# A scan's second sweep on silu in PSUM and on the state itself, with smaller pieces in the tail, in a cross-attention kernel

## The chip, the core and the metric

The kernel runs on one core of a Trainium2 chip, in float32. The time is that of one execution on the device, in microseconds (us); the times below are the median of repeated runs. Inputs lie in the chip's memory before the kernel starts, and the output is written there. The engines are called PE (TensorE, matrix products), DVE (VectorE), ACT (ScalarE), POOL (GpSimd) and SP (SyncE, which only issues transfers).

## What is computed

```python
x  = layernorm(builder_state, g1, beta1);  base_n = layernorm(base_state, g1, beta1)
x  = builder_state + mha(x, base_n, W_qkv, b_qkv, W_o, b_o)      # 8 heads of 64, softmax
xn = layernorm(x, g2, beta2)
U  = (xn @ W_in.T + b_in) @ Bmat                                  # 64 numbers a row
def step(s, u_t):
    s = silu(s @ A.T) + u_t
    return (s, s)
_, states = scan(step, zeros, U)                                  # over the rows, state of 64
out = x + states @ Cmat + (program_probs.mean(1) @ W_prog.T + b_prog)
```

There are 4096 rows of 512 and 3202 rows of keys. The last two lines are the part that the change touches.

## The kernel before

**Attention.** The rows are taken in eight blocks of 512. For each block and each pair of heads PE makes scores, ACT their exponentials, DVE adds these up, and PE multiplies them with the values; the products of several heads are then projected and normalised. The rows of a finished block are kept (`x1` in memory with the residual, `u` = U in SBUF). The last 256 rows come last: their four pairs of projection products `yb` (one bank for each of two row tiles, `last` in the plan), then `l.x1`, statistics, turning and `l.kept` for each tile.

**The scan.** Chunks of the 4096 rows run side by side: 16 steps, each on a 128x128 tile that holds 64 states of 256 chunks in two halves. The first sweep `a` starts each chunk from zero and gives the states at the chunks' ends (`end1`); the second sweep `b` starts each chunk from the end of the chunk ahead, and its states are what goes to the output. The influence of an older state fades within a chunk, and at the end the program tests that: the new ends `end0` are compared with `end1` (`differ b`), and only if an element differs by more than `TOL` (2^-21) times its row's largest does a general branch recompute everything (`tc.If(n > 0)`). The last 256 rows have a scan of their own, 20 steps on 128x32 tiles (`l.terms` puts their inputs through A, `l.z` is the product on PE, `l.h` the silu on ACT), which is compared too (`differ l`).

**How a step of a sweep is written.** Silu is written there as z/2 * (tanh(z/2) + 1). `terms` puts four steps' inputs through A into a bank ahead of time, `z` adds A times h of the step before, ACT takes the tanh, DVE makes h, which is the state without its input. In sweep `b` POOL adds the input (`states`, s = h + u), and the product with `Cmat` (`products`, four matmuls, in two column pieces of 256) gives the row's output for both halves into two banks. One half is joined with the row on DVE (`joined0`); the other is copied by ACT out of PSUM and added by POOL in two rows of three (`copied`, `added`), and joined on DVE in the third (`joined1`). Then both are stored. There are two pairs of banks, rows with even and odd number.

**What sets the order.** All of it is a list of pieces with an engine, a cost, what they come after, and a due date. `Plan.order` simulates the engines and takes on each the piece with the earliest due date that can run; the instructions are emitted in that order, and each engine runs its own in that order. The due dates are moved by the table `SHIFT` (in units of 2.15 us), an entry for each sort of piece. A piece that waits on its engine keeps the ones behind it waiting.

The names in the rows of order and profile: `z` and `za` are the banks of the sweeps, `zl` the banks of the 20 steps (the last one lies in `py_o`), `scan` the tile that holds h, s, tanh and the ends, `c_14613` and `a_t` what multiplies them, `py_o`, `py_n` and `pd_last` the output banks (`py_o` and `py_n` one pair, both halves of `pd_last` the other), `row` the row that is joined and stored, `y_l` its copy.

Of the kernel before, what the change touches and what calls it, by code (L numbers as in the profile page):

```python
# [10 lines left out]
F32 = mybir.dt.float32  # L11
# [25 lines left out]
WARM = 17  # L37
# [39 lines left out]
class Plan:  # L77
# [19 lines left out]
        "a": -42, "add": 137.25, "add.h": 196.75, "add.l": -10, "added": -29.75, "b": 2.5, "base": -5.25,  # L97
        "c2": -6.5, "close": -19, "copied": 70.25, "den": 113.25, "den.h": -32.5, "den.l": -73.25,
        "differ": -272.25, "extra": -26.25, "fall": -8.25, "fall.h": 160.75, "fall.l": 77, "fetch": 41.25,
        "fold.h": 108.75, "fold.l": 39.5, "gather": 180, "gather.h": 4.25, "gather.l": -116.5, "got": 47,  # L100
        "heads": 4, "held": -43.25, "inverse": 45.5, "inverse.h": -19.5, "inverse.l": 54, "join": -69.5,
        "join.h": -34.75, "join.l": 117.25, "joined0": -182.75, "joined1": 53, "l.copy": 43,
        "l.factors": -49.5, "l.from": -46.75, "l.h": 8, "l.idle": 264, "l.inputs": -15.75, "l.kept": -22.25,
        "l.mod": -99.25, "l.out": -7, "l.scaled": -35.75, "l.states": -41.5, "l.stats": 258.75,
        "l.store": 0.25, "l.terms": -7, "l.turn": 1, "l.x1": 16.25, "l.ys": 89.25, "l.z": -4.75, "landed": -6,
        "last": 2.25, "maximum": 76.5, "number": -17.5, "open": -0.75, "output.h": 18.25, "output.l": -14.25,
        "outs": 2.5, "outs.read": -6.75, "product": -4.25, "products": -5.75, "py1": -8.25, "q": 116,
        "query.factors": -34, "query.flip": 197, "query.load": -145.5, "query.move0": -72,
        "query.move1": 94.5, "query.move2": 13, "query.move3": 1, "query.scaled": 154.75, "query.stats": 42.5,
        "rest": -21.25, "rest.h": 110, "rest.l": -53.25, "rise": 17.25, "risen": -66.5, "row.copy": -12,  # L110
        "row.factors": -129, "row.flip": 0.75, "row.kept": -5.5, "row.load": -3.5, "row.mod": -207.5,
# [16 lines left out]
    def add(self, name, engine, cost, run, after=(), due=0, take=(), give=(), kind=None, also=0):  # L128
        assert name not in self.pieces, name
        sort = name if isinstance(name, str) else name[0]  # L130
        if sort in ("row", "query", "rows", "queries"):
            sort += "." + name[-1]
        elif sort in self.UNIT and name[1] >= self.HALVES:
            sort += ".l" if name[1] >= self.ENDS else ".h"
# [2740 lines left out]
```

## Time and profile before

| what | value |
| --- | --- |
| three runs | 1869.35, 1869.7, 1871.12 us; median 1869.7 |
| profiled execution | 1871.54 us, span on the core 1869.7 us |
| granted clock of TensorE, mean | 0.999 |
| busy over the span | PE 1853.6 (99%), DVE 1496.3 (80%), ACT 1143.1 (61%), POOL 306.0 (16%) us |
| last block's attention ends, tail begins | about 1819.5 us |
| length of the tail | 50.2 us, of which 6.7 after the last output on DVE |

The span runs from the first to the last instruction of the profiled execution, and every position in the text is counted from its start. The 99% of PE is a mean over the whole kernel, in which the tail is less than 3%. The change lies in the tail and in what is emitted just ahead of it, so the stages of the tail have to be read one by one.

### The profile page before, as it was taken

The numbers are of one execution on the slowest core, as the hardware profiler recorded it, in microseconds if no ns is written. First come the engines' busy times: TensorE is split into PE (matmuls) and PEld (weight loads), VectorE is DVE, ScalarE is ACT, GpSimd is POOL, SyncE is SP. The second block draws the span as 40 slices with busy tenths as digits, with TensorE's granted clock in tenths as the row PEclk, the third lists the DMA queues.
The fourth block names the chain that finished last, engine by engine and source line by source line (L and its number), as shares of the span: only waits on it lengthen the run. The fifth ranks groups of instructions, "written<-read, shape, count | busy, mean of one in ns | idle before, by whom it ended". The sixth has DMA issues, their size and how long they took to land.

```text
span 1869.7 us, 44352 instructions
## 1 busy us (share of the span) xinstructions
PE 1853.6 (99%) x17956; PEld 926.7 (50%) x17956; DVE 1496.3 (80%) x1734; ACT 1143.1 (61%) x1409; POOL 306.0 (16%) x395
## 2 busy tenths in 40 slices
PE   9999999999999999999999999999999999999997
PEld 5888334534353433434343435344343434577674
DVE  6642688688888889798979888888979897888776
ACT  3242577575757667575756575766757575757653
POOL 6120300021100130022102110023002210020115
PEclk9999999999999999999999999999999999999999
DMA  8663242331424233413333132423331342535577
GB/s 258 161 169 89 65 117 58 83 111 54 112 74 139 57 105 100 115 48 88 108 85 121 52 108 80 139 58 106 100 112 50 82 112 85 155 111 171 159 194 238
DMA packets 262704, 206.90 MB, mean 111 GB/s; under 512 B 95759, under 2 KB 235935, under 8 KB 262497
## 3 DMA queue, kind: packets, MB, share of 16 engines
q1 hardware_dynamic: 258476, 197.41, 37.2%
q10 hardware_dynamic: 4020, 6.62, 1.3%
q8 instruction: 143, 2.34, 0.5%
q14 instruction: 65, 0.52, 0.1%
HBM read 157.24 MB, written 29.89 MB: 100 GB/s over the span
## 4 chain that ended last, share of the span: by engine, by line
PE 97%; DVE 1%; SPq 1%; DMA 0%; ACT 0%; issue 0%; POOL 0%; ACTq 0%; DVEq 0%
PE po L1406 32%; PE s L1300 32%; PE po L1431 5%; PE s L1313 5%; PE qx L523 3%; PE pax L523 3%; PE qy L523 2%; PE pay L523 2%; PE pkx L523 2%; PE pvx L523 2%; PE pky L523 1%; PE pvy L523 1%; PE pk L863 1%; PE pv L736 1%; PE pd L1460 1%; PE pu L1920 1%
## 5 line engine op out<-in xcount | busy, mean ns | idle before, releaser
L1344 ACT ACTIVATE p<-s,shifts 128x1024 f32<-128x1024 f32 x804 | 886.2, 1110 | 437.9 <-PE s L1300 361.2
L1352 DVE TENSOR_TENSOR acc<-p,acc 128x1024 f32<-128x1024 f32 (+1 forms) x732 | 916.5, 1257 | 81.3 <-ACT p L1344 51.5
L1406 PE MATMUL po<-p,v 64*64 64x512 f32 x5600 | 730.4, 590 | 0.0
L1300 PE MATMUL s<-q,k 64*64 64x512 f32 x5600 | 729.0, 589 | 0.0
L1300 PEld LDWEIGHTS s<-q,k 64*64 64x64 f32 x5600 | 217.8, 133 | 371.1 <-issue 333.5
L1406 PEld LDWEIGHTS po<-p,v 64*64 64x64 f32 x5600 | 217.5, 133 | 360.1 <-issue 341.7
L1807 POOL TENSOR_TENSOR xr<-xr,rowb 128x512 f32<-128x512 f32 x28 | 35.7, 1276 | 793.0 <-DVE acc L1352 682.2
L1518 DVE RECIPROCAL rd<-rd 128x256 f32<-128x256 f32 (+1 forms) x64 | 109.9, 1718 | 29.7 <-ACT rd L1513 29.6
L1431 PE MATMUL po<-p,v 64*64 64x256 f32 x1600 | 107.3, 377 | 0.0
L1313 PE MATMUL s<-q,k 64*64 64x256 f32 x1600 | 106.8, 377 | 0.0
L1902 POOL TENSOR_TENSOR xr<-x,modb 128x512 f32<-128x512 f32 x28 | 35.4, 1274 | 317.2 <-DVE acc L1380 228.7
L1313 PEld LDWEIGHTS s<-q,k 64*64 64x64 f32 x1600 | 64.1, 133 | 25.1 <-issue 3.2
L1431 PEld LDWEIGHTS po<-p,v 64*64 64x64 f32 x1600 | 64.4, 133 | 21.5 <-issue 1.9
L1352 DVE TENSOR_TENSOR acc<-p,p 128x1024 f32<-128x1024 f32 x36 | 44.0, 1223 | 19.4 <-ACT p L1344 19.3
L1375 ACT COPY swap<-acc 64x512 f32<-64x512 f32 (+1 forms) x70 | 40.2, 574 | 18.8 <-DVE acc L1352 16.2
L1738 ACT ACTIVATE q<-qx,bias 128x256 f32<-128x256 f32 x42 | 17.6, 471 | 52.7 <-PE qx L523 52.7
L1588 POOL TENSOR_SCALAR rstd_x<-mv_x 128x1 f32<-128x1 f32 x28 | 24.7, 882 | 146.3 <-DVE mv_x L1585 144.6
L719 DVE TENSOR_TENSOR ks<-pky,ks 128x512 f32<-128x512 f32 x15 | 10.4, 692 | 45.0 <-PE pky L523 24.6
L1380 DVE TENSOR_TENSOR acc<-swap,acc 64x512 f32<-64x512 f32 (+1 forms) x70 | 44.1, 630 | 1.1
L713 ACT ACTIVATE ks<-pkx,bias 128x256 f32<-128x256 f32 x40 | 16.8, 471 | 43.8 <-PE pkx L523 26.6
L440 DVE TENSOR_REDUCE m<-ex 128x2 f32<-128x1024 f32 (+1 forms) x9 | 9.9, 1101 | 39.9 <-ACT ex L436 39.9
L1590 POOL TENSOR_SCALAR nm_x<-mv_x,rstd_x 128x1 f32<-128x1 f32 x28 | 34.9, 1246 | 2.8
(325 smaller groups left out, 1749.5 us busy)
## 6 DMA issues: line engine op xcount, KB each, us to landing
k<-kd SPq DMA_DIRECT2D x432, 128.0 KB, 2.6
v<-vd SPq DMA_DIRECT2D x432, 128.0 KB, 2.5
xn<-x SPq DMA_DIRECT2D x448, 32.0 KB, 1.9
xr<-in_x_dram SPq DMA_DIRECT2D x30, 256.0 KB, 4.1
x1d<-xr SPq DMA_DIRECT2D x30, 256.0 KB, 3.2
x<-in_x_dram SPq DMA_DIRECT2D x28, 256.0 KB, 3.2
cx<-in_ctx_dram SPq DMA_DIRECT2D x25, 256.0 KB, 4.0
kd<-ks SPq DMA_DIRECT2D x20, 256.0 KB, 4.9
```

The lines of the kernel that those rows point to most:

```text
L523: nc.tensor.matmul(to[:, b, :], still[:, i, b * P : (b + 1) * P], moving[:, i, :], start=(start and b == 0 and i == 0), stop=(i == 1), ski ...
L1300: nc.tensor.matmul(s[k0 : k0 + HD, a].rearrange("p b j -> p (b j)"), kts[(*w["at"][:2], c // 2)][r, b * CK + k0 : b * CK + k0 + HD], q[r], ...
L1313: nc.tensor.matmul(s[k0 : k0 + HD, a, b, :], kts[(*w["at"][:2], c)][r, b * CK + k0 : b * CK + k0 + HD], q[r], start=True, stop=True, skip_ ...
L1344: nc.scalar.activation(t[:, :, :nb, :], w["ps"][c][:, :, :nb, :], AF.Exp, bias=w["shift"])
L1352: return nc.vector.tensor_tensor(w["acc"][:, :, :nb, :], t[:, :, :nb, :], before[:, :, :nb, :], ALU.add)
L1375: nc.scalar.copy(w["swap"][r], of[(1 - k) * HD : (2 - k) * HD])
L1380: made = nc.vector.tensor_tensor(of[r], w["swap"][r], of[r], ALU.add)
L1406: nc.tensor.matmul(w["po"][k][a * HD : (a + 1) * HD], vts[Q, hp, c // 2][r, c % 2, a * HD : (a + 1) * HD], t[r, a].rearrange("p b j -> p ( ...
L1431: nc.tensor.matmul(w["po"][k][a * HD : (a + 1) * HD, :QU], vts[Q, hp, c][r, b, a * HD : (a + 1) * HD], t[r, a, b, :], start=(c == 0 and b ...
L1518: nc.vector.reciprocal(w["rd"][:, part], (w["pd"] if last else w["rd"])[:, part])
L1807: return nc.gpsimd.tensor_tensor(xs[half][:, t], xs[half][:, t], rowb, ALU.add)
L1902: return nc.gpsimd.tensor_tensor(xt[:, t], x1[:, t], modb, ALU.add)
```

## The change

- The second sweep becomes `second_sweep`. A step is: `z` = A times the whole state (no `terms`), ACT's Silu in place in PSUM, and one DVE operation s = 2 * silu + u. The state goes into one of four buffers, the last one directly into `end0`; `states` on POOL and `b.end` are gone. `z` of a step waits for the state of the step before, in place of h.
- `products` are made in four column pieces of 128, `copied` in two halves of 256 columns, each after its two pieces of the products.
- `l.terms` is made in five pieces, the four `l.idle` pairs of matmuls (which computed nothing) are gone.
- `differ` is one piece on DVE, with the absolute value as max(d, -d); it was three, the middle one on ACT.
- `l.mod` waits for `l.scaled` of the second tile, where it waited for `l.factors`. A transposed copy in the last block's last rows takes another tile (`xn2` goes). The pace of sweep `b` in the due dates is 1500 for 1900.
- `SHIFT` has entries of their own for the rows of the last block (`.e`) and for the four `last`, and nearly all its numbers for the tail are others. The order on PE is the same as before up to the third last of the 36 units of attention work.
- The general branch uses `second_sweep` too.

```diff
     SHIFT = {
-        "a": -42, "add": 137.25, "add.h": 196.75, "add.l": -10, "added": -29.75, "b": 2.5, "base": -5.25,
+        "a": 39.25, "add": 137.25, "add.h": 487.75, "add.l": 19.25, "added": -59, "b": -188.25, "base": -5.25,
...
+    def second_sweep(start, d=0, pace=0, after=()):
+
+        k = "b"
+
+        def at_(j):
+            return sv["z"][j // 4 % 2][:, j % 4, :]
+
+        def z_(j):
+            on_a(at_(j), state(j - 1) if j else sv[start][:, :NCK], start=True)
+
+        def silu_(j):
+            nc.scalar.activation(at_(j), at_(j), AF.Silu)
+
+        def s_(j):
+            nc.vector.scalar_tensor_tensor(state(j), at_(j), 2.0, u[:, j, :], ALU.mult, ALU.add)
+
+        for j in range(L):
+            yield (k, "z", j), "PE", 260, partial(z_, j), [(k, "s", j - 1)] if j else list(after), d, [], [], "quarters"
+            yield (k, "silu", j), "ACT", 280, partial(silu_, j), [(k, "z", j)] + ([] if j else ["table"]), d + 400
+            free = [("products", j - 4, part) for part in range(NC)] if j > 3 else []
+            yield (k, "s", j), "DVE", 290, partial(s_, j), [(k, "silu", j)] + free, d + 800
+            d += pace
...
-        def copied():
-            nc.scalar.activation(sv["y"][:, j % 2, :], sv["py"][j % 2][1], AF.Copy, scale=0.5)
+        def copied(half):
+            hs = slice(half * QU, (half + 1) * QU)
+            nc.scalar.activation(sv["y"][:, j % 2, hs], sv["py"][j % 2][1][:, hs], AF.Copy, scale=0.5)
...
-        nc.scalar.activation(df, df, AF.Abs)
+        nc.vector.scalar_tensor_tensor(df, df, -1.0, df, ALU.mult, ALU.max)
...
-            plan.add(("l.mod", g), "POOL", 1250, partial(mod_, g), [("l.x1", g), ("l.factors", 1)],
+            plan.add(("l.mod", g), "POOL", 1250, partial(mod_, g), [("l.x1", g), ("l.scaled", 1)],
...
-        for t in range(WARM, PRE + LT):
-            plan.add(("l.idle", t), "PE", 430, idle_, [("l.z", t), ("b", "h", L - 1)], d)
...
-            plan.add(("states", j), "POOL", 450, lambda j=j: states(j, sv["h"][j % 3]),
-                     [("b", "h", j)] + ([("products", j - 2, part) for part in range(2)] if j > 1 else []), e)
-            for part in range(2):
-                plan.add(("products", j, part), "PE", 450, partial(products_, j, part),
-                         [("states", j), *free[j % 2]], e + 1000 + part, [], [], "quarters")
+            for part in range(NC):
+                plan.add(("products", j, part), "PE", 225, partial(products_, j, part),
+                         [("b", "s", j), *free[j % 2]], e + 1000 + part, [], [], "quarters")
```

PE from the last attention products (`po`) to the end of the projection (`yb`), before. The `z` rows are sweep `b`, with `z<-u` its `terms`; `yb_17647` and `yb_17648` are row tile 0 and 1, `o_0_0` and `o_2_0` what is projected:

```order
L1431 MATMUL po_7_3_1_17388<-p_3_1_12_17529,v_3_1_12_17357 64x256
L2133 MATMUL z<-scan,a_t 64x128 x2
L2133 MATMUL z<-u,a_t 64x384 x2
L2285 MATMUL yb_17647<-wo,o_0_0_15077 128x512
L2285 MATMUL yb_17648<-wo,o_0_0_15077 128x512
L2285 MATMUL yb_17647<-wo,o_0_0_15077 128x512
L2285 MATMUL yb_17648<-wo,o_0_0_15077 128x512
L2285 MATMUL yb_17647<-wo,o_2_0_15841 128x512 x2
L2285 MATMUL yb_17648<-wo,o_2_0_15841 128x512 x2
L2133 MATMUL z<-scan,a_t 64x128 x2
L2133 MATMUL z<-u,a_t 64x512 x2
```

and the same place after, with `yb_17663` and `yb_17664` for the tiles and `pd_last<-acc` for the last sums of exponentials (`sums.35`):

```order
L1439 MATMUL po_7_3_1_17396<-p_3_1_12_17550,v_3_1_12_17368 64x256
L2141 MATMUL z<-scan,a_t 64x128 x2
L1455 MATMUL pd_last<-acc_3_1_17286,ones 64x256 x4
L2304 MATMUL yb_17663<-wo,o_0_0_15077 128x512 x2
L2304 MATMUL yb_17663<-wo,o_2_0_15841 128x512 x2
L2304 MATMUL yb_17664<-wo,o_0_0_15077 128x512 x2
L2304 MATMUL yb_17664<-wo,o_2_0_15841 128x512 x2
L2141 MATMUL z<-scan,a_t 64x128 x2
```

The `terms` are gone, tile 0 is finished with all its four products ahead of tile 1, and `sums.35` stands behind the attention's last product.

ACT around the load of the function table for tanh and silu, before. `p` are the last exponentials, `rd` are copies of sums (`den`), `scan<-z` are the tanh of sweep `b`:

```order
L1344 ACTIVATE p_3_1_11_17510<-s_3_1_11_17491,shifts 128x1024
L1344 ACTIVATE p_3_1_12_17529<-s_3_1_12_17513,shifts 128x2x256
L2161 ACTIVATE scan<-za_17026 128x128
L2385 ACT_TABLE_LOAD
L2385 ACTIVATE scan<-neg_half 128x1
L1513 ACTIVATE rd_1_1_17590,rises<-pd_1_1_0_17562 128x2x64
L1513 ACTIVATE rd_1_1_17590,rises<-pd_1_1_1_17563 128x2x64
L1513 ACTIVATE rd_2_1_17631,rises<-pd_2_1_0_17617 128x2x64
L1513 ACTIVATE rd_2_1_17631,rises<-pd_2_1_1_17618 128x2x64
L1487 COPY o_2_0_15841<-po_7_3_1_17387 128x256
L2161 ACTIVATE scan<-z 128x128 x3
L2221 ACTIVATE y_l<-py_o_17708 128x512
```

and after, where `z<-z` is the silu in place:

```order
L1352 ACTIVATE p_3_1_11_17526<-s_3_1_11_17505,shifts 128x1024
L1521 ACTIVATE rd_2_1_17540,rises<-pd_2_1_0_17529 128x2x64
L1352 ACTIVATE p_3_1_12_17550<-s_3_1_12_17535,shifts 128x2x256
L1521 ACTIVATE rd_2_1_17540,rises<-pd_2_1_1_17530 128x2x64
L2404 ACT_TABLE_LOAD
L2404 ACTIVATE scan<-neg_half 128x1
L2210 ACTIVATE z<-z 128x128 x2
L1495 COPY o_2_0_15841<-po_7_3_1_17395 128x256
L2210 ACTIVATE z<-z 128x128 x2
L2241 ACTIVATE y_l<-pd_last 128x256
```

The copies of sums are now between the last exponentials, and two steps of sweep `b` stand right behind the table load, ahead of the attention's last copy.

PE in the middle of the 20 steps, before:

```order
L2207 MATMUL py_n<-c_14613,scan 64x256
L2207 MATMUL py_o_17708<-c_14613,scan 64x256
L2133 MATMUL z<-scan,a_t 64x128 x2
L2133 MATMUL zl<-scan,c_14613 64x32 x2
L2207 MATMUL pd_last<-c_14613,scan 64x256 x8
L2133 MATMUL zl<-scan,c_14613 64x32 x2
L2207 MATMUL py_n<-c_14613,scan 64x256
```

and after:

```order
L2226 MATMUL py_o_17723<-c_14613,scan 64x128
L2141 MATMUL zl<-scan,a_t 64x128 x2
L2141 MATMUL zl<-scan,c_14613 64x32 x2
L2226 MATMUL pd_last<-c_14613,scan 64x128 x4
L2141 MATMUL z<-scan,a_t 64x128 x2
L2226 MATMUL pd_last<-c_14613,scan 64x128 x4
L2141 MATMUL zl<-scan,c_14613 64x32 x2
L2226 MATMUL pd_last<-c_14613,scan 64x128 x8
L2226 MATMUL py_n<-c_14613,scan 64x128
```

Pieces of `products` of half the width stand between the small steps, and a piece of `l.terms` (`zl<-scan,a_t`) has moved in among them.

More of the change, by code (lines that the diff above doesn't have):

```diff
@@ L102 @@
[L102 to L111, printed above, removed]
@@ L120 @@
+        "swap": -51.75, "swap.h": 3.75, "swap.l": 17.75, "table": 26, "to": -29.25, "tq": 39.25,
+        "weights": 59.75, "yb": 181.75, "l.idle": 510.75, "last": 4.75, "row.copy": -107,
+        "row.x1": 34.25, "rows.outs": 4.25, "rows.turn": 11, "states": -37.75, "fold": 21,
     }
```

180 lines of the change are left out of this document (92 added, 88 removed).

## The prediction

> **What bounds the kernel now.** I read the busy time by stage first, with stages cut where the work changes: attention of the last block, output projection of the last 256 rows, their normalisation, the chain of 20 small steps (`l.z`, `l.h`), the end, and what follows the last compute.
>
> ```profile
> core 0: us, PE busy (x) PEld busy (x) DVE busy (x) ACT busy (x) POOL busy (x), PEclk, DMA share, GB/s
> 1772.50:1819.50 47.00, 46.91 (x814) 36.90 (x812) 35.68 (x56) 28.57 (x51) 4.44 (x2) 1.00 0.66 178
> 1819.50:1826.70 7.20, 7.20 (x20) 3.07 (x20) 5.33 (x15) 0.28 (x1) 0.46 (x1) 1.00 1.07 271
> 1826.70:1836.60 9.90, 8.85 (x106) 6.09 (x110) 8.19 (x19) 3.58 (x9) 7.48 (x9) 1.00 0.79 240
> 1836.60:1858.10 21.50, 19.19 (x335) 12.73 (x330) 14.60 (x35) 10.44 (x40) 14.95 (x20) 1.00 0.74 241
> 1858.10:1863.00 4.90, 3.86 (x37) 2.14 (x36) 4.80 (x13) 1.31 (x4) 1.82 (x2) 1.00 0.97 324
> 1863.00:1869.70 6.70, 0.00 (x0) 0.00 (x0) 0.03 (x1) 0.00 (x0) 0.00 (x0) 0.68 0.47 145
> ```
>
> Up to 1819.5 PE has work in 46.91 of 47.00 us: only PE work taken out of there helps. From 1826.7 on nobody is full: PE 19.19 of 21.5, DVE 14.60, ACT 10.44, so queues and waits set the pace. The second view is the chain of waits, for what of the sweep lies on the path.
>
> ```profile
> 1818.08 0.22 PE po L1419 x8
> 1818.73 0.86 PE z L2133 x8
> 1819.59 7.06 PE yb L2285 x16
> 1826.66 1.25 PE z L2133 x8
> ...
> 1834.48 1.22 PE z L2133 x8
> 1835.70 0.87 PE zl L2133 x16
> ...
> 1842.20 0.90 PE z L2133 x4
> ...
> 1862.30 0.68 DVE xr_l L2430
> ```
>
> The four `z` pieces are the four `b.terms` (the middle two with a step in them); all stand on the path. Last, ACT's timeline and the list of waits from 1826.6 to 1863, for the pace of the 20 steps.
>
> ```profile
> 1836.62 0.23 ACT L2370 ACTIVATE scan<-zl 128x32 f32<-128x32 f32 x1 [0.60 <-PE zl L2133]
> ...
> 1839.90 0.60 ACT L2221 ACTIVATE y_l<-pd_last 128x512 f32<-128x512 f32 x1 [1.07 <-DVE row L2227]
> 1840.39 0.22 ACT L2370 ACTIVATE scan<-zl 128x32 f32<-128x32 f32 x1
> ...
> 1847.70 0.22 ACT L2370 ACTIVATE scan<-zl 128x32 f32<-128x32 f32 x1
> ...
> 1848.34 0.23 ACT L2370 ACTIVATE scan<-zl 128x32 f32<-128x32 f32 x1 [0.27 <-PE zl L2133]
> ...
> 1857.83 0.23 ACT L2370 ACTIVATE scan<-py_o 128x32 f32<-128x32 f32 x1 [0.20 <-PE py_o L2133]
> ACT y_l L2221 <- DVE row L2227: 4.6, 4, 1.2
> ACT scan L2370 <- PE zl L2133: 4.2, 9, 1.0
> ```
>
> First to last of 20 `l.h` is 1857.83 - 1836.62 = 21.2 us, 1.12 a step. An undisturbed step is 1848.34 - 1847.70 = 0.64. The rest is queueing: `copied` (`y_l`) waits 4.6 us in four places for a join on DVE to free its bank, and the next `l.h` stands behind it in ACT's queue.
>
> **The change, part by part.** The sum is made against the span of the profiled execution, 1869.7; its own time is 1871.54, and the median of the runs, 1869.7, is what I forecast with the same difference.
>
> A, up to the first `yb` product. Out goes `b.terms.0`, 0.86. In come `b.z.0`, `b.z.1`, `b.z.2`, each a pair of 64x128; the 64x128 of L1419 advances PE by 0.22, so 0.66 in all. `sums.35` only moves. Net -0.2. The new wait is that of `b.z.1` for `b.silu.0`, which must follow the table load:
>
> ```profile
> 1812.00 0.69 ACT L1344 ACTIVATE p<-s,shifts 128x512 f32<-128x512 f32 x1 [0.18 <-PE s L1313]
> ...
> 1812.87 1.28 ACT L2385 ACT_TABLE_LOAD   x1
> 1814.17 0.20 ACT L2385 ACTIVATE scan<-neg_half 128x1 f32<-128x1 f32 x1
> L2161 ACT ACTIVATE scan<-z 128x128 f32<-128x128 f32 x10 | 2.8, 281 | 1.7 <-PE z L2133 1.7
> L2168 DVE SCALAR_TENSOR_TENSOR scan<-scan,z 128x128 f32<-128x128 f32 x11 | 3.1, 283 | 5.3 <-ACT scan L2161 3.7 <-PE zl L2133 1.5
> L1518 DVE RECIPROCAL rd<-rd 128x128 f32<-128x128 f32 x2 | 1.8, 918 | 0.0
> ```
>
> From the last scores: exponential 0.69, an estimated 0.3 for one `den`, table 1.28 and 0.20, tanh's 0.28 for the silu, state 0.28, about 3.1 with a handover or two still to add; PE meanwhile has four products of 0.86 and `b.z.0`, 3.7. I take no wait; queued behind it are two attention products, so every microsecond of it would count in full, and a DVE reciprocal ahead of `b.s.0` (0.9) sets the upper end at +0.9. Silu into PSUM is not in the trace: at least the 0.23 of L2370 (a quarter of the columns), at most the 0.60 of L2221 (four times as many); I take the 0.28 of the tanh, same shape. The new state reads PSUM and SBUF as L2168 does: 0.28.
>
> B, projection: 7.06 stays. Tile 0 now finishes after four products, so its fourth comes 1.7 earlier (two of 0.86) and meets `scale.35.0`, whose two reciprocals now follow the moved `sums.35`. I count a wait of +0.3 (0 to +0.7).
>
> C, 1826.7 to the first `l.h`: `b.terms.1` and `.2`, some 0.85 each inside the 1.25 and 1.22 above, leave. But both row tiles are needed, and tile 1 hangs here:
>
> ```profile
> 1830.13 2.68 POOL L2348 TENSOR_TENSOR xr_l<-x_l,modb 128x512 f32<-128x512 f32 x2
> 1830.25 1.44 DVE L2318 TENSOR_SCALAR xh_yl<-x_l,mv_yl,rstd_yl 128x512 f32<-128x512 f32 x1
> ...
> L2200 POOL TENSOR_TENSOR scan<-scan,u 128x128 f32<-128x128 f32 x15 | 6.9, 459 | 5.4 <-PE zl L2133 1.8 <-PE py_o L2207 1.3 <-DVE scan L2168 1.1
> ```
>
> While POOL adds, this operation takes 1.44; POOL's 16 `states` (0.46 each) go, but `added.0` now stands at that place. Working the queues through to `l.terms.0` I get 9.5 for 9.9: -0.4 (0 to -1.7, both `terms`).
>
> D, the 20 steps. Out go `b.terms.3` (0.90), twelve POOL `states` on the way from state to product, and an `idle` pair. Products come in quarters of 64x128, four at 0.22, as much in sum as before; copies in halves:
>
> ```profile
> 1818.78 0.37 ACT L1487 COPY o<-po 128x256 f32<-128x256 f32 x1 [1.75 <-PE po L1431]
> 1837.72 0.69 DVE L2227 SCALAR_TENSOR_TENSOR row<-py_n,row 128x512 f32<-128x512 f32 x1 [0.94 <-PE zl L2133]
> 1838.33 0.68 DVE L2227 SCALAR_TENSOR_TENSOR row<-py_o,row 112x512 f32<-112x512 f32 x1
> ...
> 1839.12 0.68 DVE L2227 SCALAR_TENSOR_TENSOR row<-pd_last,row 128x512 f32<-128x512 f32 x1
> ```
>
> A half copy is 0.37; an `l.h` waits behind one in most steps, half of it on average: 0.64 + 0.19 = 0.83, and with PE at a quarter product when the step is ready, 0.87. 19 steps: 16.5. Floors: PE has 48 quarters (10.5), nine `b.z` (2.0), the `l.z` and two `l.terms` (about 1.6): 14.1. DVE, over D and E: 17 joins that advance it 0.61, nine states 0.20, the comparisons, `l.states` and outputs about 5: 17.2 of 21.4, tight but under it. So -4.7 (-7.1 at PE's floor; -0.9 if only `terms.3` is saved).
>
> E and F. After the last `l.h` DVE has `l.states`, two joins, one comparison, two outputs, as now: 0. The 6.7 behind the last output stay.
>
> The stores must keep up. Two windows, 1846 to 1866 and 1838 to 1867, and the median landing of the 16 stores of the shorter half rows say:
>
> ```profile
> DMA packets 3220, 5.85 MB, mean 293 GB/s; under 512 B 371, under 2 KB 371, under 8 KB 3219
> DMA packets 4112, 7.50 MB, mean 259 GB/s; under 512 B 483, under 2 KB 483, under 8 KB 4105
> ...
> out_dram<-row SPq DMA_DIRECT2D x16, 224.0 KB, 3.6
> ```
>
> From row 2 on 7.4 MB are stored (14 rows of 480 KB and 512 KB). At 293 that is 25.3 us: begun at 1835.5, done by 1860.8, about what a landing takes after my last output at 1857.8. At 259 it is 28.6, done 3.3 later. [...]
>
> Sum: -0.2 + 0.3 - 0.4 - 4.7 = -5.0, from 1869.7: 1864.7.
>
> **Rivals.** R1: the steps do not quicken, because a copy still waits for the join of two rows before (the 4.6 above), and DVE has the same joins. Then only `terms.3` and the small terms count: D -0.9, sum -1.7 with C at -0.9: 1868.0. For it: the banks are still two a side; against: DVE idles 6.9 of 21.5 there.
> R2: stores at 259 GB/s bind: 3.3 later, 1867.8.
> R3: D reaches PE's floor and DVE nearly its own: -7.1 for -4.7, 1862.1.
> R4: the new order of the last attention steps stalls PE, by the 0.9 of A and as much again among the `a.z`: 1866.3; now such waits are 0.09 of 47.
> R5, the slower side: the program ends in a comparison of the two sweeps; if one element differs by more than 2^-21 of its row's maximum, the general branch runs. Now both sweeps use the tanh form; afterwards tanh is compared with silu. At present 64 elements are compared so (`sl` against `st`, column 0) and pass, as no general branch is in the trace; afterwards 16384 are. That branch loads 32 x 4 x 26 tiles, and issuing one takes SP 0.34:
>
> ```profile
> 1830.36 0.34 SPq L2232 DMA_DIRECT2D out_dram<-row  x1
> ```
>
> so 1130 us at least: above 2990. One element decides.
> R6: without `l.idle` PE's clock falls in the chain. The clock is 1.00 in every stage with PE work and 0.68 in the 6.7 us without. Longest PE wait I find in the new order: 1.5, for tile 1 in C. At 0.68 D's 14.1 would be 20.7, +4.2: 1868.7. [...]
>
> **How the numbers follow.** No change is what lies within 0.2%, 3.7 us. Forecast 1864.7 (its own range 1862.5 to 1866): 0.47. R3 0.12, R1 0.17, R2 0.08, R4 0.08, R5 0.03, R6 0.05 (0.03 of it as slow as the halved clock). Faster: forecast and R3, 0.59, and a part of R4, 0.61. Slower: R5, the 0.03 of R6, and 0.02 for several waits together, 0.08. Same 0.31. The range 1860.5 to 1869.5 takes in R1 to R4 and leaves out the slower cases and the best of R3.
>
> **What would show it.** Right: four `yb` of one tile in a row; first `l.h` near 1836, last near 1852.5; its steps mostly under 0.9; the last output near 1857.8; PE at clock 1.00 until then. Wrong in A: a gap on PE ahead of the second `z` or behind 1800. Wrong in D: `y_l` still waiting for `row` for microseconds, or DVE full with joins. Wrong about the stores: DMA share 1.0 to the end with landings far above 3.6 us. Instructions of the general branch would mean R5.

## The result, and the profile after

The changed kernel takes 21282.28 us (21269.77 to 21288.74, 6 runs) against 1870.41 us before (1869.34 to 1871.62, 6 runs): 11.378 times as long, with an interval of 11.363 to 11.393. The general branch runs. It is the rival R5 that the prediction gave 0.03. The profiled execution took 21269.77 us, its span is 21268.0.

Four of the stages of the prediction, of the kernel after, and behind them the three parts of the branch (the columns are those of the prediction's table: engines, clock, transfers):

```profile
core 0: us, PE busy (x) PEld busy (x) DVE busy (x) ACT busy (x) POOL busy (x), PEclk, DMA share, GB/s
1772.50:1819.50 47.00, 46.58 (x850) 41.42 (x848) 36.55 (x55) 30.98 (x53) 4.43 (x2) 1.00 0.63 178
1826.70:1836.60 9.90, 9.56 (x174) 7.19 (x174) 7.57 (x18) 3.73 (x11) 6.28 (x6) 1.00 0.82 252
1836.60:1858.10 21.50, 17.96 (x488) 15.51 (x482) 14.31 (x30) 11.08 (x45) 10.12 (x8) 1.00 0.79 264
1858.10:1863.00 4.90, 2.84 (x38) 1.25 (x38) 3.88 (x11) 0.96 (x3) 1.31 (x2) 0.77 0.65 216
1866.00:14681.00 12815.00, 10123.78 (x28928) 5450.59 (x28928) 2585.28 (x8418) 4460.02 (x14912) 67.44 (x192) 0.51 0.12 35
14681.00:20757.00 6076.00, 2829.90 (x16386) 1200.22 (x16386) 1234.88 (x4356) 1401.74 (x4353) 0.00 (x0) 0.50 0.00 0
20757.00:21268.00 511.00, 205.17 (x708) 141.75 (x708) 132.77 (x616) 62.36 (x295) 13.90 (x11) 0.50 0.10 32
```

Up to 1866 the kernel does what it did before, in about the same time. Then it recomputes: 12815 us of attention, 6076 us of the sweep, made again in 256 rounds so that each chunk can follow the one ahead, and 511 us of outputs and last rows. Two starts of a round in the middle part show its price, 23.7 us; each round begins with a load of ACT's function table:

```profile
15022.12 1.28 ACT L2210 ACT_TABLE_LOAD   x1 [1.48 <-PEq L2803]
...
15045.83 1.28 ACT L2210 ACT_TABLE_LOAD   x1 [1.48 <-PEq L2803]
```

So there are two questions: why the two sweeps no longer agree, and what the tail would have been worth if they did. The tail is to be seen in this very trace, ahead of the branch. The table has the kernels before and after and the runs e5 to e15. Its last five columns are from the profiled execution: the time from the start of the main loop's 601st exponential to the first `yb` product, from there to the first `l.h`, the 20 steps from first to last start, from there to the end of the last output on DVE, and from there to the end of the span. The medians are of 11 runs from e5 on, against runs of the kernel before on the same chip (medians 1871.28 us for e5 to e8, 1870.78 for e9 to e12, 1871.54 for e13 to e15); e1 to e4, which carry counters, ran once each and stand below.

| kernel | median us | ratio to before (interval) | loop to `yb` | to `l.h` | 20 steps | to last output | to end |
| --- | --- | --- | --- | --- | --- | --- | --- |
| before | 1870.41 | | 415.8 | 17.1 | 21.2 | 5.1 | 6.8 |
| after | 21282.28 | 11.378 (11.363 to 11.393) | 416.2 | 16.4 | 20.1 | 7.3 | - |
| e5 | 1870.33 | 0.9994 (0.9985 to 1.0003) | 416.0 | 16.4 | 20.1 | 7.2 | 4.8 |
| e6 | 1867.10 | 0.9981 (0.9971 to 0.9990) | 418.6 | 16.2 | 16.5 | 4.3 | 8.4 |
| e7 | 1868.14 | 0.9989 (0.9980 to 0.9999) | 416.0 | 16.4 | 20.0 | 5.3 | 6.9 |
| e8 | 1875.06 | 1.0024 (1.0015 to 1.0033) | 415.1 | 17.6 | 19.8 | 9.1 | 7.9 |
| e9 | 1868.83 | 0.9993 (0.9984 to 1.0002) | 416.2 | 16.4 | 20.1 | 6.2 | 4.8 |
| e10 | 1870.44 | 0.9999 (0.9990 to 1.0008) | 418.4 | 16.4 | 17.5 | 8.3 | 6.5 |
| e11 | 1868.85 | 0.9992 (0.9983 to 1.0001) | 416.0 | 16.4 | 20.2 | 6.2 | 4.8 |
| e12 | 1868.90 | 0.9995 (0.9986 to 1.0004) | 416.0 | 16.4 | 17.9 | 8.2 | 6.6 |
| e13 | 1869.11 | 0.9988 (0.9979 to 0.9997) | 417.0 | 16.4 | 20.7 | 5.6 | 5.0 |
| e14 | 1869.33 | 0.9992 (0.9983 to 1.0001) | 416.0 | 16.4 | 20.8 | 5.7 | 5.0 |
| e15 | 1867.08 | 0.9983 (0.9974 to 0.9992) | 416.0 | 16.4 | 18.3 | 6.2 | 5.0 |

The first of these columns differs by 2.6 us between executions whose attention stands in the same order (e5 and e6), so the others are the ones to compare. The traces put a part of it into gaps inside one group of products on PE, in which PE waits for nothing that the profile shows: 1.75 us ahead of 1814.30 in e10, 1.25 us ahead of 1822.40 in e6. Each of these two gaps ends 1.3 to 1.4 us behind a 16 KB packet of the instruction queue; whether the one has to do with the other, no run tests. The columns are of one execution each, and those of e6, e7 and e10 took 1.8 to 3.2 us more than their medians. By the intervals, e6 and e7 (which leave work out), e13 and e15 are faster than the kernel before and e8 is slower, all by less than 0.4%; e5, e9 to e12 and e14 can't be told from it.

### The profile page after: what moved, and what is told of

Its sections match the earlier page's. It is cut to its first block, busy times and chain, and to the rows that moved or that the text cites. A ratio compares the mean times of both kernels' runs of the same rounds, so it can differ in the third digit from the quotient of the medians.

```text
span 21268.0 us, 207640 instructions
## 1 busy us (share of the span) xinstructions
PE 15010.5 (71%) x64204; PEld 7726.7 (36%) x64204; DVE 5448.9 (26%) x15124; ACT 7068.0 (33%) x20977; POOL 380.2 (2%) x582
## 5 line engine op out<-in xcount | busy, mean ns | idle before, releaser
L2141 PE MATMUL z<-scan,a_t 64*64 64x128 f32 x16512 | 2847.6, 443 | 3249.2 <-DVE scan L2213 2759.9
L2705 PE MATMUL pd_last<-row,row 64*128 64x256 f32 (+1 forms) x6656 | 3919.2, 690 | 199.9 <-ACT row L2706 185.3
L2729 PE MATMUL py_o<-row,row 128*64 128x128 f32 x12800 | 3599.4, 435 | 313.1 <-ACT row L2724 313.1
L2721 PE MATMUL py_n<-ident,row 128*128 128x128 f32 (+1 forms) x6656 | 2333.0, 446 | 1601.8 <-DVE row L2717 1601.8
L2707 DVE TENSOR_REDUCE row<-row 128x1 f32<-128x256 f32 (+2 forms) x3584 | 1401.2, 391 | 7035.8 <-ACT row L2706 7035.8
L2729 PEld LDWEIGHTS py_o<-row,row 128*64 128x64 f32 x12800 | 2265.7, 217 | 2216.8 <-ACT row L2724 2166.6
L2724 ACT COPY row<-py_n 128x256 f32<-128x256 f32 (+2 forms) x3584 | 1277.6, 356 | 4953.9 <-PE py_n L2721 4953.9
L2705 PEld LDWEIGHTS pd_last<-row,row 64*128 64x128 f32 x6656 | 1647.7, 307 | 1399.2 <-issue 865.6
L2706 ACT COPY row<-pd_last 128x256 f32<-128x256 f32 (+2 forms) x3584 | 1255.8, 350 | 2437.2 <-PE pd_last L2705 2437.2
L2711 ACT ACTIVATE row<-row,row 128x256 f32<-128x256 f32 (+2 forms) x3584 | 1682.6, 472 | 22.3 <-DVE row L2709 21.1
```

The lines of the kernel that those rows point to most:

```text
L2141: nc.tensor.matmul(z[r], a[r, r], right[r], stop=True, skip_group_check=True, **how)
L2705: nc.tensor.matmul(ps, q4[h, hp, :], kc[h], start=True, stop=True)
L2706: nc.scalar.copy(s(c), ps)
L2707: nc.vector.tensor_reduce(tops[:, c : c + 1], s(c), AX.X, ALU.max)
L2711: nc.scalar.activation(s(c), s(c), AF.Exp, bias=top, accum_out=dens[:, c : c + 1])
L2721: nc.tensor.transpose(banks[2][:n, b * P : (b + 1) * P], s(c)[:, b * n : (b + 1) * n], ident)
```

## Experiments: why the branch runs

**e1 and e2** put counters between the tail and the branch, in the changed kernel and in the one before (the code is shortened):

```diff
+    for each test (new, old), for power in (-2, -1, 0, 1, 2, 3, 5):
+        nc.vector.tensor_scalar(ok, df, 2.0**-power, sv["top"], ALU.mult, ALU.is_gt)
+        nc.vector.tensor_reduce(seen[:, k : k + 1], ok, AX.X, ALU.add)
...
+        for i, least in enumerate((0, 3, 15, 63, 255, 1023, 4095)):
+            with tc.If(c > least, label=f"more_{k}_{i}"):
+                nc.vector.memset(sv["df"][:, : 8 * k + i + 1], 0.0)
```

> The changed kernel, with counters put between its tail and the branch: for each comparison the number of elements that differ by more than 2^-21 of the row's maximum times a power of two, each shown as a ladder of empty writes (more than 0, 3, 15, 63, 255, 1023, 4095 elements; the write's width is 8 times the counter's number plus the step). Counters 0 to 6: chunk ends at 2^-23, -22, -21, -20, -19, -18, -16; 7 to 10: last 256 rows at 2^-22, -21, -20, -19; 11: the softmax guard. Theory F (silu of the table against the tanh form): counter 2 between 4 and 4000 of 16384, counter 4 nearly empty, 8 and 11 empty; time 21.3 ms and some 100 us. Theory R (rounding, since A is now applied to the whole state and not to input and h apart): the same counters, but few, under 64, and counter 3 empty. Theory L (the last rows' comparison fails): counter 8 not empty, counter 2 empty. Theory C (the comparison itself, now on one engine, counts wrong): counter 2 empty, yet the branch runs.

> The kernel before with the same counters: all theories expect counters 2, 8 and 11 empty and no general branch, so 1870 us and what the counters cost (50 to 150 us). What it tells: counters 0 and 1 say how near the limit the tanh form on both sides stands. Theory F: counter 0 (2^-23) a few to some hundred, counter 1 (2^-22) near empty. Theory C: counter 2 not empty although the branch stays away.

e1 took 21320.98 us. Its ladder, from DVE's timeline (the width of the write is the code; the last row is the branch):

```profile
1876.93 0.06 DVE L2826 MEMSET scan<- 128x1 f32 x1 [0.97 <-DVE scan L2821]
1877.48 0.06 DVE L2826 MEMSET scan<- 128x2 f32 x1 [0.49 <-DVE scan L2826]
1877.97 0.06 DVE L2826 MEMSET scan<- 128x3 f32 x1 [0.43 <-DVE scan L2826]
1878.44 0.06 DVE L2826 MEMSET scan<- 128x4 f32 x1 [0.41 <-DVE scan L2826]
1881.13 0.07 DVE L2826 MEMSET scan<- 128x9 f32 x1 [2.63 <-DVEq L2825]
1881.60 0.07 DVE L2826 MEMSET scan<- 128x10 f32 x1 [0.41 <-DVE scan L2826]
1882.05 0.07 DVE L2826 MEMSET scan<- 128x11 f32 x1 [0.39 <-DVE scan L2826]
1884.74 0.07 DVE L2826 MEMSET scan<- 128x17 f32 x1 [2.62 <-DVEq L2825]
1921.73 0.30 DVE L2761 MEMSET scan<- 128x129 f32 x2 [36.91 <-DVEq L2825]
```

Widths 1 to 4: 64 to 255 elements of the chunk ends differ by more than 2^-23 of their row's largest. 9 to 11: 16 to 63 by more than 2^-22. 17 and no 18: one to three elements of 16384 by more than the limit, 2^-21. No 25: none by more than twice the limit. The last rows and the softmax guard (from 57 on) are clean, so theory L falls. Between F and R e1 alone does not decide: one to three elements are fewer than the 4 that F expected at least, and R allows them. e2 took 1919.89 us and wrote nothing at all: before, no element is beyond 2^-23, a quarter of the limit (F had expected some there).

**e3** gives the changed kernel's second sweep the tanh form, **e4** gives the old second sweep silu from the table (shortened):

```diff
e3  -            nc.scalar.activation(at_(j), at_(j), AF.Silu)
e3  +            nc.scalar.activation(sv["h"][j % 3], at_(j), AF.Tanh, scale=0.5)
e3  -            nc.vector.scalar_tensor_tensor(state(j), at_(j), 2.0, u[:, j, :], ALU.mult, ALU.add)
e3  +            nc.vector.scalar_tensor_tensor(h, h, 1.0, at_(j), ALU.add, ALU.mult)
e3  +            nc.vector.tensor_tensor(state(j), h, u[:, j, :], ALU.add)
e4  -            nc.scalar.activation(sv["th"][j % 2], at_(j), AF.Tanh, scale=0.5)
e4  +            nc.scalar.activation(sv["th"][j % 2], at_(j), AF.Silu)      # sweep b alone
e4  -            h = (th + 1) * z
e4  +            h = 2 * th                                                  # sweep b alone
```

> The changed kernel, but its second sweep makes silu from tanh as the first one does (two operations on DVE in place of one); A is still applied to the whole state, and the pieces and dates are those of the change. Theory F: counter 2 empty and no branch, so about 1871 us and 50 to 150 us of counters. Theory R: counter 2 not empty and 21.3 ms. Theory C: 21.3 ms with counter 2 empty.

> The kernel before, but its second sweep takes silu from the table in place of tanh (and doubles it on DVE); input products, POOL's additions, pieces, dates and the comparison are as before. Theory F: counter 2 as full as in the changed kernel, within a factor of two, and the general branch, some 21 ms. Theory R and C: counter 2 empty, no branch, about 1870 us and 50 to 150 us of counters.

e3 took 1927.72 us, no branch; its ladder ends with the third write:

```profile
1879.75 0.06 DVE L2828 MEMSET scan<- 128x1 f32 x1 [0.95 <-DVE scan L2823]
1880.31 0.06 DVE L2828 MEMSET scan<- 128x2 f32 x1 [0.50 <-DVE scan L2828]
1880.78 0.06 DVE L2828 MEMSET scan<- 128x3 f32 x1 [0.41 <-DVE scan L2828]
```

16 to 63 elements beyond 2^-23, none beyond 2^-22: that is what A on the whole state does by rounding, and it stays at half the limit or under. e4 took 22549.72 us, with the same eight widths as e1 and the branch behind them. So theory F is shown both ways, though its numbers for e1 and e2 were too high: the function decides, not the form of the product (R) and not the comparison (C). How far apart the two ways to silu end is read from the ladder of e1: the largest difference lies between 2^-21 and 2^-20 of its row's largest, between the limit and twice the limit. How accurate tanh or silu is by itself, no run shows.

**e11** asks whether the test could have been kept: silu from the table in steps 0 to 13, tanh in the last two (and the comparisons in PSUM, as in e9 below).

```diff
+            if j < L - 2:
+                nc.scalar.activation(at_(j), at_(j), AF.Silu)
+            else:
+                nc.scalar.activation(sv["h"][j % 3], at_(j), AF.Tanh, scale=0.5)
```

> The changed kernel with its own limit of 2^-21, with silu from the table in steps 0 to 13 of the second sweep and the tanh form in steps 14 and 15, and with the comparisons in PSUM as in e9. Theory F with fading (what two ways to silu differ by in an early step has faded by the end; the last steps' difference is what is compared): no general branch, time within 1 us of e9, so 1868 to 1871. Rival (the difference gathers over all steps): the branch, above 21 ms.

1868.85 us and no branch, within 0.1 of e9. With these inputs two steps are enough for the early steps' differences to fade below the limit. How far below is not shown, as e11 has no counters; nor does a run show that the comparison in PSUM, at 2^-21, still catches a second sweep with silu from the table throughout.

## Experiments: what the tail is worth

**e5** changes one number, the limit.

```diff
-TOL = 2.0**-21
+TOL = 2.0**-20
```

> The changed kernel with TOL 2^-20 for 2^-21 and nothing else: by the counters no element is beyond that, so the general branch stays away and the time is that of the tail alone. Theory T (the tail as its trace ahead of the branch shows it): measured from the 601st exponential of the main loop, the last output ends 0.8 later than before (1864.75 - 1404.78 against 1862.97 - 1403.76), so 1870 to 1872, not to be told from the kernel before. Theory G (the forecast's sum, with the branch's start disturbing the trace): 1864.7.

Theory T: the same as before, within 0.15% either way. The forecast's 5 us are not there, branch or no branch. Two waits of e5 from the list of waits between 1826.6 and 1866, where before `copied` waited 4.6 for joins:

```profile
ACT y_l L2241 <- PE pd_last L2226: 6.5, 8, 2.7
ACT y_l L2241 <- PE py_o L2226: 3.3, 7, 0.6
```

The half copies now wait for their own products, 9.8 us in all in that window and 5.0 of it (2.8 and 2.2) between 1836.5 and 1858.5, where the 20 steps lie, with an `l.h` behind them in ACT's queue.

**e6** leaves ACT's copies out for rows 2 to 15; **e10** keeps them, and lets `l.h` go first where a copy stands right ahead of it:

```diff
e6  +            if j < 2:
e6                   nc.scalar.activation(sv["y"][:, j % 2, hs], ...)
e10 +        for one, two in list(zip(moved, moved[1:])):      # neighbours in ACT's order
e10 +            if str(one[0])[:6] == "copied" and two[0] == "l.h":
e10 +                ...
e10 +                if not any(one in p["after"] for p in pieces[a + 1 : b + 1]):
e10 +                    pieces.insert(b, pieces.pop(a))
```

> As e5, but ACT's copies are left out for rows 2 to 15 (POOL adds the copies of rows 0 and 1 again, so that the second halves of these rows are not what they should be); PE, DVE and POOL have the same pieces in the same order. Theory P (a step of the 20 waits on ACT behind a copy that waits for its products): 20 steps in 13 to 17 us for 20.1, time 3 us or more under e5. Theory V (DVE's list after the last state of the second sweep sets the end): steps as under P, but the time falls by 1.5 at most. Theory Q (PE's products alone set the pace): steps within 1 us of 20.1, time within 1 us of e5.

> As e5, but where a half copy stands right ahead of a step l.h in ACT's order and nothing in between needs the copy, the two change places; no work is left out. Theory P (the step waits behind a copy that waits for its products): 20 steps in 15 to 18 us for 20.1, time 1 to 2.5 under e5. Theory Q (PE's products between the steps set the pace, wherever the copy stands): steps within 1 us of 20.1, time within 0.7 of e5.

First and last `l.h` on ACT's timeline, of e5, e6 and e10:

```profile
1836.80 0.23 ACT L2389 ACTIVATE scan<-zl 128x32 f32<-128x32 f32 x1 [0.18 <-PE zl L2141]
...
1856.93 0.23 ACT L2389 ACTIVATE scan<-py_o 128x32 f32<-128x32 f32 x1 [0.54 <-PE py_o L2141]
```

```profile
1839.15 0.23 ACT L2390 ACTIVATE scan<-zl 128x32 f32<-128x32 f32 x1 [0.83 <-PE zl L2141]
...
1855.63 0.23 ACT L2390 ACTIVATE scan<-py_o 128x32 f32<-128x32 f32 x1 [0.54 <-PE py_o L2141]
```

```profile
1838.14 0.23 ACT L2389 ACTIVATE scan<-zl 128x32 f32<-128x32 f32 x1 [1.06 <-PE zl L2141]
...
1855.65 0.23 ACT L2389 ACTIVATE scan<-py_o 128x32 f32<-128x32 f32 x1 [0.30 <-PE py_o L2141]
```

20.1 us fall to 16.5 without copies and to 17.5 by the exchange: theory P holds for the steps. For the time it holds only in e6 (3.2 under e5). e10 gains nothing: what the steps save, 2.6, comes back behind them, 1.1 up to the last output and 1.6 from there to the end. Something else ends the tail; e12 below shows what. Without copies the steps hang on PE instead: in e6 `l.h` waits 8.5 us for it (2.1 in e5), and PE has work in 15.82 of the 16.48 us.

e6 also shows the next bound. Its transfers by windows, and those of the kernel before (the last two numbers are the share and GB/s):

```profile
1838.00:1848.00 10.00, 9.97 (x304) 9.41 (x296) 7.61 (x18) 4.16 (x18) 10.00 (x10) 1.00 0.91 305
1848.00:1856.00 8.00, 7.37 (x220) 6.57 (x216) 6.50 (x17) 2.90 (x13) 1.13 (x1) 1.00 0.92 297
1856.00:1862.00 6.00, 2.09 (x37) 0.95 (x26) 3.87 (x13) 0.19 (x1) 0.00 (x0) 0.85 0.96 321
1862.00:1864.00 2.00, 0.00 (x0) 0.00 (x0) 0.00 (x0) 0.00 (x0) 0.00 (x0) 0.50 1.02 341
1864.00:1868.40 4.40, 0.00 (x0) 0.00 (x0) 0.00 (x0) 0.00 (x0) 0.00 (x0) 0.50 0.12 33
```

```profile
1838.00:1848.00 10.00, 8.96 (x154) 5.57 (x146) 6.04 (x13) 4.91 (x19) 6.37 (x10) 1.00 0.54 180
1848.00:1856.00 8.00, 7.33 (x138) 5.00 (x142) 6.07 (x16) 3.98 (x16) 6.41 (x9) 1.00 0.95 313
1856.00:1862.00 6.00, 5.28 (x59) 3.13 (x50) 5.82 (x16) 2.46 (x8) 3.85 (x4) 1.00 0.95 315
1862.00:1865.00 3.00, 0.07 (x3) 0.00 (x0) 1.03 (x3) 0.00 (x0) 0.00 (x0) 1.00 0.95 298
```

In e6 the transfers are nine tenths full from 1838 to 1864, while compute ends at 1860.0; the end comes 8.4 behind it. Before, they were full from 1848 to 1865. In e5 there is room between 1856 and 1862:

```profile
1856.00:1862.00 6.00, 3.25 (x71) 2.00 (x64) 4.95 (x12) 1.57 (x6) 2.33 (x2) 1.00 0.61 197
```

**e7** leaves out POOL's additions for rows 2 to 15, **e9** keeps them and moves the comparisons' differences to PSUM:

```diff
e7  +            if j < 2:
e7                   nc.gpsimd.tensor_tensor(row(1), ...)
e9  -        top, df, ok = sv["top"], sv["df"][:, :n], sv["ok"][:, :n]
e9  +        top, df, ok = sv["top"], sv["z"][0][:, 1, :n], sv["z"][0][:, 2, :n]
e9  -        nc.vector.scalar_tensor_tensor(df, df, -1.0, df, ALU.mult, ALU.max)
e9  +        nc.vector.tensor_reduce(df, df.unsqueeze(2), AX.X, ALU.max, apply_absolute_value=True)
```

> As e5, but POOL's additions are left out for rows 2 to 15 (the second halves of the spread rows are stored without the scan's part); copies and all else stay. Theory O (operations of DVE that read and write SBUF alone last as long as an addition on POOL runs beside them): the operations of 1.29 and 1.22 us of e1 (the state ahead of the last rows, the first comparison) take 0.2 to 0.3, and the last output comes 1.5 to 2.5 earlier. Theory J (the last joins wait for PE and ACT, not for DVE): the operations shorten, but the time stays within 0.7 of e5.

> As e5 (limit doubled), but the two comparisons keep their differences and marks in a free PSUM bank (absolute value by a reduction over one element), and the state ahead of the last rows is written there too; pieces, dates and order stay. Theory O (only operations of DVE between SBUF and SBUF are held by POOL): the comparison's operation of 1.20 us in e5 takes 0.3, and the one of 1.30, which still reads SBUF alone, does too if writing to PSUM is enough; last output 1 to 2 us earlier, time 0.5 to 2 us under e5. Rival (any operation of DVE is held): both stay above 1, time within 0.5 of e5.

e5, DVE and POOL around the first comparison: two operations last until the addition beside them has ended.

```profile
1854.22 1.30 DVE L2393 SCALAR_TENSOR_TENSOR scan<-scan 128x32 f32<-128x32 f32 x1
1856.46 1.20 DVE L2275 TENSOR_SCALAR scan<-scan 128x128 f32<-128x128 f32 x1
...
1854.17 1.27 POOL L2244 TENSOR_TENSOR row<-y_l,row 112x512 f32<-112x512 f32 x1 [1.75 <-ACT y_l L2241]
1856.31 1.26 POOL L2244 TENSOR_TENSOR row<-y_l,row 112x512 f32<-112x512 f32 x1 [0.88 <-ACT y_l L2241]
```

e9, the same two, the second of which now reads PSUM:

```profile
1852.01 1.30 DVE L2393 SCALAR_TENSOR_TENSOR z<-scan 128x32 f32<-128x32 f32 x1
1854.26 0.36 DVE L2275 TENSOR_SCALAR z<-z,scan 128x128 f32<-128x128 f32 x1
...
1851.97 1.26 POOL L2244 TENSOR_TENSOR row<-y_l,row 112x512 f32<-112x512 f32 x1 [1.75 <-ACT y_l L2241]
1854.11 1.27 POOL L2244 TENSOR_TENSOR row<-y_l,row 112x512 f32<-112x512 f32 x1 [0.88 <-ACT y_l L2241]
```

Without the additions (e7) the second one takes 0.29, and the first one 0.20:

```profile
1854.73 0.29 DVE L2276 TENSOR_SCALAR scan<-scan 128x128 f32<-128x128 f32 x1
```

So 1.20 becomes 0.36 in e9 with POOL still adding; the one that reads two tensors of SBUF stays at 1.30, wherever it writes. Theory O holds as far as the inputs go; that writing to PSUM would free the other one was wrong. The two of e5 end 0.08 and 0.09 us behind the addition beside them (1855.52 and 1857.66 for 1855.44 and 1857.57), L2393 of e9 also 0.08; L2275 of e9 ends at 1854.62, while its addition goes on to 1855.38. To the last output e9 has 6.2 for 7.2, e7 5.3. The median of e7 is 2.2 under e5, that of e9 1.5, but e9's ratio to its own runs of before is that of e5 within 0.0001, so a gain of e9 in time is not shown.

**e8** puts the old due dates and the old pace under the new structure (the table and `B_PACE` alone are edited).

> As e5, but with the table of due dates and the pace of the kernel before (new sorts take the number of the old sort that they come from). Theory N (the re-dating carries what the structure gains): 3 us or more slower than e5. Theory S (the structure sets the pace, the dates little): within 1.5 us of e5.

4.7 us slower than e5, and slower than the kernel before by 0.24%: theory N. The structure under dates that were made for another one loses; the new dates bring it back to even.

**e13** moves the first comparison behind the joins of rows 12 to 15 (by this the second one falls behind the last outputs). What speaks for it is e5's chain of waits:

```profile
1857.90 0.69 DVE row L2247
1858.59 0.04 issue
1858.63 1.15 PE pd_last L2226 x32
...
1860.48 0.39 ACT y_l L2241
1860.87 0.02 issue
1860.89 0.69 DVE row L2247
```

The join at 1857.90 frees the bank for the last row's products. It stands on DVE behind L2393 and the six operations of the comparison, which begin at 1854.22.

```diff
-            ("b", ..., NCK, "bad", [("b", "s", L - 1)]),
+            ("b", ..., NCK, "bad", [("b", "s", L - 1), *(joins of rows 12 to 15)]),
```

> As e5 (limit doubled), but the first comparison comes after the joins of rows 12 to 15. Only DVE's order changes: the six operations of the comparison move behind five joins, and the last outputs stand ahead of the second comparison. Theory B (in e5 a join that frees the bank of the last row stands behind 4.3 us of the state, and of the comparison, on DVE): that join starts at once, PE's last products and the copies come 2 us or more earlier, the last output 2 to 4 us earlier from the main loop, time 1 to 3 under e5. Theory W (the stores' rate sets the end): last output as under B, time within 0.7 of e5. Theory K (DVE is full to the end, the order of its work is worth nothing): last output within 1 us.

> e11 (own limit of 2^-21, tanh in the last two steps, comparisons in PSUM) with the comparison behind the joins. Theory B: 1 to 2.5 under e11's 1868.85, so 1866.3 to 1867.9 and faster than the kernel before by 0.1 to 0.25%. Theory W: within 0.7 of e11.

The DVE timeline of e13 at that place:

```profile
1854.38 1.29 DVE L2393 SCALAR_TENSOR_TENSOR scan<-scan 128x32 f32<-128x32 f32 x1
1856.08 0.69 DVE L2247 SCALAR_TENSOR_TENSOR row<-pd_last,row 128x512 f32<-128x512 f32 x1 [0.40 <-issue]
...
1859.74 0.69 DVE L2247 SCALAR_TENSOR_TENSOR row<-pd_last,row 128x512 f32<-128x512 f32 x1 [0.46 <-ACT y_l L2241]
```

The join comes 1.7 us after L2393 starts, for 3.7 in e5, and the last one 5.4 for 6.7. From the first `yb` product to the last output e13 takes 42.8 us for 43.8: theory K's "within 1 us", where B wanted 2 to 4. The median is 1.2 under e5, B's lower end, but in another set of runs. e14 against e11 gains nothing (1869.33 and 1868.85), as theory W had it. So this order alone is worth about 1 us on the way to the last output in e13, and nothing in e14.

**e12 and e15** take the edits together: e12 is e11 with the exchange of e10, e15 also has the comparison behind the joins.

> e11 with the exchange of e10. If the gains of e9 and e10 add: 1866 to 1868.5, faster than the kernel before by 0.1 to 0.25%. If the stores' rate binds from here on (transfers fill 0.9 and more of their engines from 1828 to 1864 in e6): not under 1867, whatever the last output gains. If neither e9 nor e10 gains: 1870 to 1872.

> e14 with the steps ahead of the copies as in e10. If the 20 steps set the end once the comparison is out of the way: 1 to 2 under e14. If the rows do (products, copies, joins in two pairs of banks): within 0.5 of e14.

From first `yb` product to last output: e5 43.8, e11 42.8, e12 42.6, e14 43.0, e15 41.0. Neither the exchange (e12) nor the comparison's place (e14) gains on e11 alone; both together give 1.8. The last row's products on PE show why, in e12 and in e15:

```profile
1855.21 1.10 PE L2234 MATMUL pd_last<-c,scan 64*64 64x128 f32 x32 [2.94 <-DVE row L2255]
```

```profile
1854.09 1.10 PE L2234 MATMUL pd_last<-c,scan 64*64 64x128 f32 x32 [0.60 <-ACT y_l L2249]
```

In e12 the steps are done sooner, but PE then waits 2.94 us for the join behind the comparison (1.74 in e5, 2.52 in e10, 0.91 in e11). With the join ahead of the comparison the wait is 0.60. These are two paths of like length: the 20 steps, and the rows with their banks and DVE's comparison. e12's 1868.90 lies between "the gains add" (up to 1868.5) and "neither gains" (from 1870). e15 is 2.25 under e14, a little more than the 1 to 2 that were expected if the 20 steps set the end.

The semaphores in the traces show what the end of the span hangs on. Before, in e5 to e9 and in e11 it comes 1.5 to 1.6 us behind the last landing of a store. In e13 to e15 the stores have landed 2.1 to 2.6 before the end, and it comes 3.4 behind the number on which the branch is decided, as the second comparison now stands behind the last outputs: there the comparison is the next thing to shorten. In e10 and e12 SP at last waits 0.9 and 0.8 us for ACT, whose first instruction behind the branch comes 3.5 and 3.6 after it (0.4 in e5); what ACT waits for is not shown. So e10 and e12 lose a part of their gain to a wait that no edit aimed at.

e15 keeps the limit of 2^-21 and is faster than the kernel before: 1867.08 us, ratio 0.9983 (0.9974 to 0.9992). Its interval ends just under no change; it is the best of the versions that leave nothing out.

## Why the prediction was wrong

**The step that failed** is the weighing of R5. The mechanism, the place and the limit were right (tanh form against silu, 2^-21, one element decides), and 1864.7 would have needed that none of 16384 elements is beyond it. The chance of 0.03 had nothing on record behind it but 64 elements of the last rows that compare silu with tanh and pass today. They say almost nothing: at one to three in 16384 (e1), 64 elements hold 0.004 to 0.012 on average, if the differences are spread alike, and pass nearly always. For 256 times as many elements a row was needed on how large the differences are, and there was none; no number on record spoke for 0.03 rather than for a far higher chance. The bound "above 2990" was a bound by SP's issues alone; the branch cost 19402 us, mostly by attention on PE at a clock of 0.51 and by the serial sweep.

**The sum behind it** was also wrong: e5, with the branch away, can't be told from the kernel before (0.9 us under it by the medians, with an interval of the ratio that takes in 1), where -5.0 was forecast. Term by term, from the table (e5 less before, in the profiled executions, -1.4 in all):

- A, forecast -0.2, measured +0.2: the three `b.z` and the moved `sums.35` cost what they save. R4's 0.9 twice is not there.
- B and C, forecast -0.1, measured -0.7: right in direction, inside the range of C. With the old dates the stretch stays longer (17.6 in e8), so the new dates bring it; that it is tile 0 finished ahead of tile 1 is not shown by itself.
- D, forecast -4.7, measured -1.1: 1.06 a step, not 0.87. The step that failed is "an `l.h` waits behind one in most steps, half of it on average": it waits behind the copy and behind the copy's own wait for its two quarters of the products, 5.0 us within the steps, as much as the copies waited for joins before (4.6). R1 had the wrong wait, but nearly the right outcome. That e6 has the forecast's 16.5 is luck: e6 has no copies to wait behind, and by the forecast's own numbers its steps (0.87 less 0.19) would be at PE's floor of 14.1. PE has work there in 15.82 of 16.48 us, so that floor was too low as well.
- E, forecast 0, measured +2.1: the comparison as one piece on DVE stands ahead of a join (about 1, e13), and two of the operations there are held by POOL's additions (1.30 and 1.20 us for 0.20 and 0.29 in e7; about 1 to the last output with one of them freed, e9; 2 without additions, e7). The two causes don't add up: e14 has both edits and is no better to the last output than e11, which has e9's without e13's. The prediction had quoted a row of that kind (1.44 beside POOL's 2.68; the other tile's took 0.55 at 1827.54 with no addition beside it) and used it in C alone.
- F, forecast 0, measured -1.9: before, the transfers were full to 1865 and the end hung on them. In e5 they were 0.61 full between 1856 and 1862. The last store lands 3.2 us behind the last output, for 5.2 before, and the end comes 1.6 behind the landing in both. This is R2's mechanism; it hid part of E's loss, and in e6 it takes back half of what compute gains (6.8 us less from the first `yb` product to the last output, 3.6 more from there to the end).
- The clock (R6): 1.00 through the steps of e5 without `l.idle`, as forecast; there it falls behind the last outputs' products alone (0.81 from 1862.5 to 1863, then 0.50). In the kernel after it is 0.50 from 1860.7 on (0.77 in the windows above), in e10 and e12, with PE waits of 2.5 and 2.9 us ahead of the last row's products, from 1858.8 and 1856.7 on, with the last outputs' products still to come: a fall as in R6, but behind the steps. The 0.03 for a clock that is halved in the steps is a term that no run shows: from 1836 to 1860 the windows of e5 to e8 have 1.00.
- R2, R3, R4 and the 1868.7 of R6 are counted from 1864.5 and not from the sum's 1864.7, so each is 0.2 too low.

What stays open: how the 1 to 3 us between e5 and e13 to e15 divide, since the intervals of those ratios overlap; what PE and ACT wait for in the gaps that the profile puts down to nothing; and whether other inputs would pass the test of e11 to e15, as all runs have the same.

## What to carry to other kernels

A test that guards a slow path is part of the fast path's price: an edit that makes the same function in another way (silu for tanh) must be weighed by how many elements are compared and how near the limit they lie, and a small sample that passes says almost nothing on that. Here the same way in the last two steps on both sides was enough to pass at the old limit. In a tail with several paths of like length, count what an instruction waits for as well as how long it lasts, put bookkeeping behind what frees a buffer, and don't drop an edit because it shows nothing alone: e12 and e14 gained nothing, e15 did.

## What the runs showed of the hardware

- Silu from ACT's table and silu from its tanh differ, after 16 steps of a scan, by more than 2^-22 of the row's largest in 16 to 63 of 16384 elements and by more than 2^-21 in one to three (e1, e4); rounding alone (e3) stays at 2^-22 or under.
- In e5 a DVE operation with two SBUF inputs (L2393, 128x32) and a 128x128 scalar operation from SBUF to SBUF (L2275) took 1.30 and 1.20 us and ended 0.08 and 0.09 behind the addition that POOL ran beside them; without additions (e7) they took 0.20 and 0.29. With a PSUM input, the second took 0.36 beside an addition (e9). A scalar operation on one column took 0.15 beside one (at 1861.73 in e5).
- In the branch's attention (1866 to 14681, kernel after) the clock was 0.51 on average, with PE busy for 10123.8 of 12815 us: the trace has 51 stretches of 3.4 or 6.8 us at 1.00 there, 208 us in all (the first from 1884.6), and 0.50 otherwise. In the serial sweep (14681 to 20757) it was 0.50 throughout.
- In e10, with a PE wait of 2.52 us ahead of the last row's products, the clock was 0.50 from 1858.8 on, and the last outputs' products (64x512) took 1.22 and 1.06 us. In the kernel after, with a wait of 1.74, it was 0.50 from 1860.7 on, and they took 0.75 and 1.06. In e5, with the same wait of 1.74, it was 1.00 to 1862.5, and they took 0.69 and 0.59. What makes it fall is not shown.
